# Layer 2's LayerNorm computed by token rows, and most of it placed beside the first image's attention

## The chip, the cores and the metric

The kernel runs on one core of a Trainium2 chip. The metric is the time of one execution on the device in microseconds (us). Five engines of the core have queues of their own: TensorE (PE; its weight loads are shown as PEld), VectorE (DVE), ScalarE (ACT), GpSimd (POOL) and SyncE (SP, which only issues transfers). On each engine instructions run in the order of its queue, and semaphores make them wait for other engines.

## The reference, cut to what matters

A batch of 4 images with 256 channels and 32 x 32 positions passes four layers. Layer 0 is a state-space block, layer 1 an attention-like convolution, layer 2 attention and a mixture of experts, layer 3 linear attention and an LSTM-like recurrence over 1,024 steps. The change lies between the end of layer 0 and the end of layer 2's attention:

```python
def _ln_t(v, eps=1e-5):
    m = jnp.mean(v, axis=-1, keepdims=True)
    s = jnp.var(v, axis=-1, keepdims=True)
    return (v - m) / jnp.sqrt(s + eps)

# layer 1: f = theta phi / N ; y = f g ; w_y = conv1x1(y), normalised over the batch
    return w_y + x
# layer 2
t = _to_tokens(x)                     # (4, 1024, 256): a token is a position
t = t + _L2_attn_ref(_ln_t(t), ...)   # one head of width 256, softmax over 1024 tokens
t = t + _L2_ffn_ref(_ln_t(t), ...)    # the experts
```

Because theta, phi and g of layer 1 have one output channel, its output w_y is, for each channel, a scale and an offset applied to one row theta of the image. The scale and offset need statistics over all four images; with them, the residual of one image does not depend on the others. Layer 2's LayerNorm and attention are independent for each image.

## The kernel before, in words

The activations x stay in SBUF with channels on the partitions: two chunks of 128 channels, 4 images, 1,024 positions each (`s.x`). All arithmetic is in fp32. T is 4,096 tokens; `NBLK` = 8 blocks of W = 512 tokens; `TPI` = 8 tiles of 128 tokens in an image; `BPI` = 2 blocks of 512 in an image.

*Order of the work.* The kernel is written on a framework that inserts the semaphores and lists each engine's instructions in an order of its own, within the dependencies. `_in_order` adds ordering without a semaphore between the instructions of one engine. Tiles come from pools with a number of buffers (`bufs`); a new tile in a used buffer waits for the readers of the old one, and so does a tile of a new pool in memory that a closed pool had. [...]one tile `[P, W]` is a bank. Two engines that read the same PSUM tile do so one after the other, in the order of the source.

*Layer 1* (`_layer1`, L546 to L659). TensorE forms theta, phi and g rows (L582), ScalarE and VectorE take statistics (L586 to L594), a product with ones sums them over the partitions (L605), and some thirty small VectorE instructions give the offset `off` and the coefficient `coef` (L610 to L644), among them `_rsqrt`, a reciprocal root in 13 steps. Then, image by image, the theta row is spread over the partitions by a product (L649), scaled by ScalarE into `wy` (L654), and added to x by VectorE (L659).

*Layer 2's LayerNorm* (`_layernorm`, L190 to L222) works with channels on the partitions. For each of the eight blocks a product with 1/256 gives the mean on all partitions (L202), VectorE subtracts it (L203), ScalarE squares (L205), and a second product collects the variance of the block in one of eight rows (L207). After the last block, ScalarE takes the root (L215), VectorE the reciprocal (L217), and for each block a product spreads the row over the partitions (L221) and VectorE multiplies (L222). The result is `u`, for all images.

*Layer 2's weights* (`_layer2_weights`, L678) are combined by small products (L703 to L709) and copied by VectorE (L710 to L717) while layer 1 ends.

*Layer 2's attention* (`_layer2_attention`, L759 to L860). For each image: four blocks of queries (L789, copied by ScalarE at L794), eight tiles of values (L801, L805), then eight tiles of 128 queries. A tile has four score products (L814), a row maximum on VectorE (L822 to L824), the exponential on ScalarE (L828), the division on VectorE (L832, L833), and eight transposes in two groups of four (L838), one copied by ScalarE (L845) and one by VectorE (L843). After four tiles, two times eight products with the values (L850) and an addition to x (L855). Score tiles `p_s`, transposed tiles `p_t` and the other products `p_mm` have two PSUM tiles each, eight banks together.

Beside the attention of images 1 to 3 goes the routing head of the image before (`_head`), a generator: after each step it yields, and `beside(n)` in the attention loop takes n steps, 11 for each tile of 128 queries and so 88 in an image. What is left is taken at the image's end (L856). Image 0 has no such parts: L778 gives it an empty iterator. The head begins with transposes of x into token rows (L874), statistics (L877, L880) and a copy into `rows` (L878).

*The experts* (`_layer2_experts`) follow, with transfers issued by POOL; small tables for them are computed by VectorE (`_table`, `_pick`, `_count`, `_part_tiles`), in tiles of the pool `m.one`. Layer 3 comes last and is the longest part.

Of the kernel before, what the change touches and what calls it, by code (L numbers as in the profile page):

```python
# [11 lines left out]
F32 = mybir.dt.float32  # L12
# [7 lines left out]
P = 128  # L20
B = 4
# [62 lines left out]
def _setup(s):  # L84
# [30 lines left out]
    s.avg_row = s.const.tile([P, 2 * NBLK - 1], F32, name="avg_row")  # L115
    nc.vector.memset(s.avg_row, 0.0)
    nc.vector.memset(s.avg_row[:, NBLK - 1 : NBLK], 1.0 / D)

    s.spread = s.const.tile([NBLK, NBLK, P], F32, name="spread")
    nc.vector.tensor_copy(s.spread, _bc(s.ident[:NBLK, :NBLK], 2, P))  # L120

# [68 lines left out]
def _layernorm(s, u):  # L190

    nc = s.nc
    with ExitStack() as ctx:
        pool = ctx.enter_context(s.tc.tile_pool(name="ln", bufs=2))
        ps = ctx.enter_context(s.tc.tile_pool(name="ln_ps", bufs=2, space=PSUM))
        ps1 = ctx.enter_context(s.tc.tile_pool(name="ln_ps1", bufs=1, space=PSUM))
        var = ps1.tile([NBLK, W], F32, name="var")
        for i in range(NBLK):
            t = bass.ts(i, W)
            mean = ps.tile([P, W], F32, name="mean")  # L200
            for k in range(C):
                nc.tensor.matmul(mean, s.avg, s.xt[:, k, t], start=k == 0, stop=k == C - 1)  # L202
            nc.vector.tensor_sub(u[:, :, t], s.xt[:, :, t], _bc(mean, 1, C))  # L203
            sq = pool.tile([P, C, W], F32, name="sq")
            nc.scalar.activation(sq, u[:, :, t], AF.Square)  # L205
            for k in range(C):
                nc.tensor.matmul(  # L207
                    var,
                    s.avg_row[:, NBLK - 1 - i : 2 * NBLK - 1 - i],
                    sq[:, k, :],  # L210
                    start=i == 0 and k == 0,
                    stop=i == NBLK - 1 and k == C - 1,
                )
        std = pool.tile([NBLK, W], F32, name="std", bufs=1)
        nc.scalar.activation(std, var, AF.Sqrt, bias=s.eps[:NBLK])  # L215
        rstd = pool.tile([NBLK, W], F32, name="rstd", bufs=1)
        nc.vector.reciprocal(rstd, std)  # L217
        for i in range(NBLK):
            t = bass.ts(i, W)
            wide = ps.tile([P, W], F32, name="wide")  # L220
            nc.tensor.matmul(wide, s.spread[:, i, :], rstd, start=True, stop=True)  # L221
            nc.vector.tensor_mul(u[:, :, t], u[:, :, t], _bc(wide, 1, C))  # L222
# [323 lines left out]
def _layer1(s):  # L546
# [4 lines left out]
    with ExitStack() as ctx:  # L551
        keep = ctx.enter_context(tc.tile_pool(name="l1_keep", bufs=1))
        pool = ctx.enter_context(tc.tile_pool(name="l1", bufs=2))
        ps = ctx.enter_context(tc.tile_pool(name="l1_ps", bufs=1, space=PSUM))
        wide = ctx.enter_context(tc.tile_pool(name="l1_wide", bufs=2, space=PSUM))
# [13 lines left out]
        spread = keep.tile([P, B, P], F32, name="spread")  # L569
# [4 lines left out]
        rows = keep.tile([P, BPI, W], F32, name="rows")  # L574
        stats = keep.tile([P, BPI, nc.vector.BN_STATS_DIM], F32, name="stats")
        dot = keep.tile([P, BPI], F32, name="dot")
        for i in range(BPI):
            p = [ps.tile([P, W], F32, name=f"p_{j}") for j in range(2)]
            for j in range(2):
                for k in range(C):  # L580
                    for b in range(B):
                        nc.tensor.matmul(  # L582
                            p[j][bass.ts(b, R), :], w[:, j, k, :], s.x[:, k, b, bass.ts(i, W)],
                            start=k == 0, stop=k == C - 1, tile_position=(0, R * b),
                        )
            nc.scalar.activation(rows[:, i, :], p[0], AF.Identity, bias=bias)  # L586
            nc.vector.bn_stats(stats[:, i, :], rows[:, i, :])
            prod = pool.tile([P, W], F32, name="prod")
            nc.vector.scalar_tensor_tensor(
                prod, p[1], s.row["g_b"], rows[:, i, :], ALU.add, ALU.mult,  # L590
                accum_out=dot[:, i : i + 1],
            )
# [11 lines left out]
        p = ps.tile([P, 3, B], F32, name="p_own")  # L604
# [30 lines left out]
        coef = keep.tile([P, B, C], F32, name="coef")  # L635
        nc.vector.tensor_mul(coef, _bc(d, 2, C), _bc(scale, 1, B))

        off = keep.tile([P, C], F32, name="off")
# [7 lines left out]
        for b in range(B):  # L646
            theta = wide.tile([P, BPI, W], F32, name="theta")
            for i in range(BPI):
                nc.tensor.matmul(  # L649
                    theta[:, i, :], spread[:, b, :], rows[:, i, :], start=True, stop=True  # L650
                )
            for c in range(C):
                wy = pool.tile([P, L], F32, name="wy")
                nc.scalar.activation(  # L654
                    wy, theta.rearrange("p i w -> p (i w)"), AF.Identity,
                    bias=off[:, c : c + 1], scale=coef[:, b, c : c + 1],
                )
                xs = s.x[:, c, b, :]
                nc.vector.tensor_add(xs, xs, wy)  # L659
# [60 lines left out]
def _layer2(s):  # L720
# [4 lines left out]
    with ExitStack() as ctx:  # L725
# [28 lines left out]
        m.counts = None  # L754
        _layer2_attention(s, m)
# [3 lines left out]
def _layer2_attention(s, m):  # L759
    nc, tc = s.nc, s.tc  # L760
    scale = D**-0.5
    with ExitStack() as ctx:
        keep = ctx.enter_context(tc.tile_pool(name="l2_keep", bufs=1))
        u = keep.tile([P, C, T], F32, name="u")
        with tc.tile_pool(name="l2_w", bufs=1) as w_pool:
            with tc.tile_pool(name="l2_w_ps", bufs=1, space=PSUM) as w_ps:
                w = _weights(s, w_pool, "w_l2")
                _layernorm(s, u)
# [8 lines left out]
        for b in range(B):  # L777
            parts = _head(s, m, b - 1, psum) if b > 0 else iter(())  # L778
# [264 lines left out]
def _table(s, m, name, n, tiles):  # L1043
# [5 lines left out]
    t = lambda shape, x: m.one.tile(shape, F32, name=f"{name}_{x}")  # L1049
# [15 lines left out]
def _pick(s, m, name, mine, values):  # L1065
# [3 lines left out]
    w = m.one.tile([P, n, K], F32, name=f"{name}_w")  # L1069
    nc.vector.tensor_mul(w, mine, _bc(values, 1, n))  # L1070
    of = m.one.tile([P, n], F32, name=f"{name}_of")
# [4 lines left out]
def _weight_rows(s, m, name, expert):  # L1076
# [3 lines left out]
    row = m.one.tile([P, n], F32, name=f"{name}_row")  # L1080
# [6 lines left out]
def _count(s, m, name, values, n, size, least):  # L1087

    nc = s.nc
    edges = m.one.tile([P, n], F32, name=f"{name}_edges")  # L1090
    nc.vector.tensor_scalar(edges, m.marks[:, :n], float(size), float(least), ALU.mult, ALU.add)
    over = m.one.tile([P, E, n], F32, name=f"{name}_over")
    nc.vector.tensor_tensor(over, _bc(values, 2, n), _bc(edges, 1, E), ALU.is_ge)
    held = m.one.tile([P, E], F32, name=f"{name}_count")
# [4 lines left out]
def _taken(s, m, name, n, first, tiles):  # L1099

    nc = s.nc
    taken = m.one.tile(list(tiles.shape), F32, name=f"{name}_taken")
# [5 lines left out]
def _first_tiles(s, m):  # L1108
# [7 lines left out]
    base = m.one.tile([P, E], F32, name="f_base")  # L1116
# [11 lines left out]
def _part_tiles(s, m, name, n, A, tiles, start, ahead):  # L1128
# [9 lines left out]
    if K > E:  # L1138
        over = m.one.tile([P, n], F32, name=f"{name}_over")
# [5 lines left out]
    base = m.one.tile([P, K], F32, name=f"{name}_base")  # L1145
# [4 lines left out]
    at = m.one.tile([P, n, A], F32, name=f"{name}_at")  # L1150
    nc.vector.tensor_tensor(at, _bc(own, 2, A), _bc(s.token[:, :A], 1, n), ALU.add)
    counts = m.one.tile([P, K], F32, name=f"{name}_counts")
# [4 lines left out]
    valid = m.one.tile([P, n, A], F32, name=f"{name}_valid")  # L1157
# [15 lines left out]
    places = m.one.tile([P, n * A], F32, name=f"{name}_ahead")  # L1173
# [8 lines left out]
def _other_tiles(s, m):  # L1182
# [5 lines left out]
    tiles = m.one.tile([P, 2 * E], F32, name="m_tiles")  # L1188
    start = m.one.tile([P, 2 * E], F32, name="m_start")
# [8 lines left out]
    begin = m.one.tile([P, E], F32, name="h_start")  # L1198
# [4 lines left out]
    left = m.one.tile([P, E], F32, name="h_left")  # L1203
# [3 lines left out]
    total = m.one.tile([P, 1], F32, name="h_total")  # L1207
# [7 lines left out]
def _layer2_experts(s, m):  # L1215
# [9 lines left out]
    with ExitStack() as body:  # L1225
        wp = body.enter_context(tc.tile_pool(name="moe_w", bufs=2))
        hp = body.enter_context(tc.tile_pool(name="moe_h", bufs=2))
        rp = body.enter_context(tc.tile_pool(name="moe_r", bufs=3))
# [367 lines left out]
def _layer3_lstm(s, x, u_l3, lam, q, wq, constants):  # L1596
# [295 lines left out]
    _setup, _layer0, _layer1, _layer2, _layer3,  # L1892
# [92 lines left out]
```

## Time and profile before

| what | us |
|---|---|
| median of 3 runs (3392.86 to 3399.31) | 3398.27 |
| the profiled execution, its own time | 3408.06 |
| its span, first to last instruction | 3406.3 |
| layer 1's first product to its offset | 343.06 to 359.10 |
| layer 1's residual, all images | 359.1 to 370.2 |
| layer 2's LayerNorm, all images | 370.2 to 422.2 |
| attention of image 0 | 422.2 to 508.2 |
| attention of image 1, with image 0's head | 508.2 to 596.4 |
| attention of image 2, with image 1's head | 596.4 to 685.2 |

Over the whole span TensorE is busy 93%, VectorE 59%, ScalarE 36%, POOL 11%. The mean granted TensorE clock is 0.973 of full speed. All durations below come from one profiled execution. In the tables of stages, a number in brackets after x is a count of records; an fp32 matmul is recorded twice and a transpose once. The chain of waits follows the work that ended last from instruction to instruction back through what released each. A line in a group table ends with the idle time of the engine just before such instructions and what ended it.

### The profile page before, as it was taken

Reading aid. Unit: us, or ns where it says so; the run is one execution under the profiler, and the core shown is the slowest. Engines: PE = TensorE matmul, PEld = TensorE weight load, DVE = VectorE, ACT = ScalarE, POOL = GpSimd, SP = SyncE. Lnnn points to the kernel's source line nnn. Section 1 sums busy time; section 2 is a strip of 40 time slices with the busy share of each in tenths; the row PEclk is TensorE's granted clock in tenths of the full one; section 3 lists DMA queues with packets and bytes.
Section 4 is the critical chain, followed back from the end, with each engine's and each line's share of the span. In section 5 each row is a group of like instructions: output and inputs, shape, how many; then the busy total and the mean of one; then the engine's idle time right before and its main releaser. Section 6 shows DMA issues by size and latency. Waiting matters only on the chain.

```text
span 3406.3 us, 146430 instructions
## 1 busy us (share of the span) xinstructions
PE 3177.1 (93%) x65186; PEld 2489.1 (73%) x65186; DVE 1997.0 (59%) x8389; ACT 1233.9 (36%) x5057; POOL 378.8 (11%) x468
## 2 busy tenths in 40 slices
PE   7788899998899996999999999999999999999888
PEld 4465344446788884688888888888888888888776
DVE  5696534452211115557777777776777767776666
ACT  4633222223222222433434334343343343443333
POOL 0083002223433330000000000000000000000000
PEclk9899899999999997999999999999999999999999
DMA  1291001115555654000000000000000000000000
GB/s 69 67 298 34 10 0 38 38 36 203 187 195 206 230 212 148 0 3 5 4 11 4 5 11 4 11 4 4 11 4 5 10 4 5 10 5 4 10 4 10
DMA packets 78058, 180.50 MB, mean 53 GB/s; under 512 B 6256, under 2 KB 63920, under 8 KB 72816
## 3 DMA queue, kind: packets, MB, share of 16 engines
q0 software_dynamic: 14880, 106.99, 8.5%
q1 hardware_dynamic: 60624, 59.12, 5.9%
q8 instruction: 511, 8.37, 1.0%
q10 hardware_dynamic: 1920, 5.00, 0.4%
q14 instruction: 123, 1.01, 0.1%
HBM read 111.26 MB, written 59.84 MB: 50 GB/s over the span
## 4 chain that ended last, share of the span: by engine, by line
PE 72%; DVE 14%; ACT 5%; issue 3%; DMA 2%; POOL 1%; ACTq 0%; DVEq 0%; POOLq 0%
PE p_c L1826 11%; PE p_c L1817 8%; PE ph L1300 6%; PE po L1334 6%; DVE turned L1867 6%; PE p_i L1817 5%; PE p_o L1826 5%; PE p_i L1826 5%; PE p_o L1817 5%; PE beside L1767 4%; PE p_mm L850 3%; PE p_s L814 2%; ACT a_o L1868 2%; DVE x L1880 2%; ACT th L1878 1%
## 5 line engine op out<-in xcount | busy, mean ns | idle before, releaser
L1868 ACT ACTIVATE add<-turned 128x8 f32<-128x8 f32 x1024 | 214.3, 209 | 1011.4 <-DVE turned L1867 1011.4
L1826 PE MATMUL p_c<-w_v,x 128*4 128x64 f32 x16368 | 416.7, 219 | 60.6 <-DVE x L1880 57.9
L1817 PE MATMUL p_c<-xg,shift 128*128 128x64 f32 x2048 | 446.0, 299 | 0.0
L1826 PE MATMUL p_o<-w_v,x 128*4 128x64 f32 x16368 | 417.8, 219 | 0.0
L1826 PE MATMUL p_i<-w_v,x 128*4 128x64 f32 x16368 | 417.4, 219 | 0.0
L1817 PE MATMUL p_i<-xg,shift 128*128 128x64 f32 x2048 | 407.7, 281 | 0.0
L1867 DVE STREAM_TRANSPOSE turned<-p_c 128x64 f32<-128x64 f32 x1024 | 255.7, 250 | 253.9 <-PE p_c L1826 220.0
L1817 PE MATMUL p_o<-xg,shift 128*128 128x64 f32 x2048 | 396.4, 275 | 0.0
L1817 PEld LDWEIGHTS p_c<-xg,shift 128*128 128x128 f32 x2048 | 304.9, 188 | 117.6 <-DVE turned L1867 0.4
L1826 PEld LDWEIGHTS p_c<-w_v,x 128*4 128x4 f32 x16368 | 227.9, 85 | 180.8 <-DVE x L1880 102.0
L1880 DVE TENSOR_TENSOR x<-a_o,th 128x8 f32<-128x8 f32 x1024 | 171.2, 167 | 246.0 <-ACT th L1878 246.0
L1817 PEld LDWEIGHTS p_o<-xg,shift 128*128 128x128 f32 x2048 | 311.4, 192 | 0.0
L1817 PEld LDWEIGHTS p_i<-xg,shift 128*128 128x128 f32 x2048 | 305.1, 188 | 0.0
L1826 PEld LDWEIGHTS p_o<-w_v,x 128*4 128x4 f32 x16368 | 281.9, 87 | 0.8 <-issue 0.5
L1826 PEld LDWEIGHTS p_i<-w_v,x 128*4 128x4 f32 x16368 | 281.6, 87 | 0.3
L1867 DVE STREAM_TRANSPOSE turned<-p_i 128x64 f32<-128x64 f32 x1024 | 271.9, 266 | 0.9 <-PE p_i L1826 0.7
L1292 ACT ACTIVATE hT<-ph,w 128x256 f32<-128x256 f32 (+1 forms) x288 | 131.3, 465 | 355.8 <-PE ph L1300 267.3
L1300 PE MATMUL ph<-uT,w 128*128 128x256 f32 x1056 | 241.6, 386 | 19.6 <-DVE uT L1279 11.3
L1867 DVE STREAM_TRANSPOSE turned<-p_o 128x64 f32<-128x64 f32 x1024 | 255.6, 250 | 0.9 <-PE p_o L1826 0.3
L1334 PE MATMUL po<-w,hT 128*128 128x256 f32 x1104 | 251.1, 380 | 2.7 <-ACT hT L1292 1.5
L1868 ACT ACTIVATE a_o<-turned 128x8 f32<-128x8 f32 x1024 | 213.3, 208 | 95.4 <-DVE cell L1871 4.5
L1300 PEld LDWEIGHTS ph<-uT,w 128*128 128x128 f32 x1056 | 203.2, 194 | 50.2 <-DVE uT L1279 12.1
(499 smaller groups left out, 4395.0 us busy)
## 6 DMA issues: line engine op xcount, KB each, us to landing
sorted<-zeros SPq DMA_DIRECT2D x32, 1032.0 KB
y_in<-results SPq DMA_DIRECT2D x16, 512.0 KB
x<-in_x_dram SPq DMA_DIRECT2D x8, 512.0 KB
tokens<-rows SPq DMA_DIRECT2D x4, 1024.0 KB
x<-tokens SPq DMA_DIRECT2D x8, 512.0 KB
out_dram<-x_l SPq DMA_DIRECT2D x64, 64.0 KB
results<-y,place POOLq DMA_INDIRECT x69
w_l<-in_w_l_dram ACTq DMA_DIRECT2D x1, 1092.0 KB
```

The costliest lines, as they stand in the source:

```text
L814: nc.tensor.matmul(p_s[:, h, :], q[:, k, q0 : q0 + P], u[:, k, b * L + h * W : b * L + (h + 1) * W], start=k == 0, stop=k == C - 1,)
L850: nc.tensor.matmul(p, v[:, n, bass.ts(c, P)], prT[:, n, :], start=n == 0, stop=n == TPI - 1,)
L1292: nc.scalar.activation(hT[:, n, : A * P], ph, AF.Gelu, bias=b1[:, n : n + 1])
L1300: nc.tensor.matmul(ph, w1[:, k, bass.ts(n, P)], uT[:, k, :], start=k == 0, stop=k == C - 1,)
L1334: nc.tensor.matmul(po, hT[:, n, bass.ts(a, P)], w2[:, n, :], start=n == 0, stop=n == NHC - 1,)
L1767: nc.tensor.matmul(p[bass.ts(i, R), :], rows[:, k, bass.ts(g, R)], w_u[:, k, at : at + GQ // GC], start=k == 0, stop=k == C - 1, tile_posi ...
L1817: nc.tensor.matmul(p[:, :H], shift[:, row * B : row * B + P], xg[n][:, g, bass.ts(i, H)], start=True, stop=t == 0,)
L1826: nc.tensor.matmul(p[R * i : R * i + B, :H], hs[:, t - 1, bass.ts(k, B)], w_v[:, k, i * GQ + g * H : i * GQ + (g + 1) * H], start=False, s ...
L1867: nc.vector.transpose(zt.rearrange("p c w -> p (c w)"), pz[g][:, :H])
L1868: nc.scalar.activation(dst.rearrange("p (c b) -> p c b", c=C), zt[:, :, :B], f)
L1878: nc.scalar.activation(th, cell[:, :, 1], AF.Tanh)
L1880: nc.vector.tensor_mul(h, a_o, th)
```

## The change

*Layer 2's LayerNorm* becomes `_norm_parts`, a generator for one image. It transposes two tiles of 128 tokens at a time into one PSUM tile, so that tokens are on the partitions; ScalarE copies the rows to SBUF, VectorE takes mean and variance of each row (`bn_stats`, `bn_aggr`). After four such groups come `_rsqrt` on all eight tiles at once and the negative product of mean and root (`shift`); ScalarE scales the eight tiles of rows in place; they are transposed back in four groups of four, and VectorE copies each to `u`. `rows` is the tile that the heads use too, from `m.one`, with one buffer.

*Layer 1* no longer adds its residual. It returns a generator `parts(b, psum)` that does so for one image in two halves of 512 positions. What this needs later (`l1_spread`, `l1_rows`, `l1_coef`, `l1_off`) lies in a pool `norm` that lives through the attention. `_layer1` is now called from `_layer2_attention`, after the load of layer 2's weights is issued; it is no longer a phase of its own.

*Placement.* Image 0's residual and norm run ahead of the attention, in four PSUM tiles of their own, with VectorE's instructions held in the order of the source. Those of images 1 to 3 become the parts beside image 0's attention, where there were none: 28 steps an image, 84 in all, in the banks of `p_mm`.

*Tables.* The small tables of the experts go to a pool `m.tables`, which is `m.one` for the first tiles and a pool of the experts' stage afterwards. The constants `avg_row` and `spread` of the old norm go.

```diff
-    s.avg_row = s.const.tile([P, 2 * NBLK - 1], F32, name="avg_row")
-    nc.vector.memset(s.avg_row, 0.0)
-    nc.vector.memset(s.avg_row[:, NBLK - 1 : NBLK], 1.0 / D)
-
-    s.spread = s.const.tile([NBLK, NBLK, P], F32, name="spread")
-    nc.vector.tensor_copy(s.spread, _bc(s.ident[:NBLK, :NBLK], 2, P))
...
-def _layernorm(s, u):
...
+def _norm_parts(s, pool, one, u, b, psum):
+    nc = s.nc
+    mv = pool.tile([P, TPI, 2], F32, name="mv")
+    rows = one.tile([P, TPI, 2, ROW], F32, name="rows")[:, :, 0, :D]
+    for n in range(0, TPI, 2):
+        p = psum()
+        for i in range(2):
+            for k in range(C):
+                at = i * D + k * P
+                nc.tensor.transpose(
+                    p[:, at : at + P], s.x[:, k, b, bass.ts(n + i, P)], s.ident
+                )
+        yield
+        nc.scalar.copy(rows[:, n : n + 2, :], p.rearrange("p (n d) -> p n d", n=2))
+        stats = pool.tile([P, 2, nc.vector.BN_STATS_DIM], F32, name="stats")
+        for i in range(2):
+            nc.vector.bn_stats(stats[:, i, :], p[:, bass.ts(i, D)])
+        for i in range(2):
+            nc.vector.bn_aggr(mv[:, n + i, :], stats[:, i, :])
+        yield
+    rstd = pool.tile([P, TPI], F32, name="rstd")
+    for i, _ in enumerate(_rsqrt(s, pool, rstd, mv[:, :, 1])):
+        if i % 4 == 3:
+            yield
+    shift = pool.tile([P, TPI], F32, name="shift")
+    nc.vector.scalar_tensor_tensor(shift, mv[:, :, 0], -1.0, rstd, ALU.mult, ALU.mult)
+    yield
+    for n in range(TPI):
+        nc.scalar.activation(
+            rows[:, n, :], rows[:, n, :], AF.Identity,
+            bias=shift[:, n : n + 1], scale=rstd[:, n : n + 1],
+        )
+        if n % 4 == 3:
+            yield
+    for i in range(BPI):
+        for c in range(C):
+            p = psum()
+            for j in range(TPB):
+                nc.tensor.transpose(
+                    p[:, bass.ts(j, P)], rows[:, i * TPB + j, bass.ts(c, P)], s.ident
+                )
+            yield
+            nc.vector.tensor_copy(u[:, c, b * L + i * W : b * L + (i + 1) * W], p)
+            yield
...
-def _layer1(s):
+def _layer1(s, after):
...
-        for b in range(B):
-            theta = wide.tile([P, BPI, W], F32, name="theta")
-            for i in range(BPI):
-                nc.tensor.matmul(
-                    theta[:, i, :], spread[:, b, :], rows[:, i, :], start=True, stop=True
-                )
+    def parts(b, psum):
+        for i in range(BPI):
+            p = psum()
+            nc.tensor.matmul(p, spread[:, b, :], rows[:, i, :], start=True, stop=True)
+            yield
+            wy = after.tile([P, C, W], F32, name="wy", bufs=2)
             for c in range(C):
-                wy = pool.tile([P, L], F32, name="wy")
                 nc.scalar.activation(
-                    wy, theta.rearrange("p i w -> p (i w)"), AF.Identity,
+                    wy[:, c, :], p, AF.Identity,
                     bias=off[:, c : c + 1], scale=coef[:, b, c : c + 1],
                 )
-                xs = s.x[:, c, b, :]
-                nc.vector.tensor_add(xs, xs, wy)
+            yield
+            xs = s.x[:, :, b, bass.ts(i, W)]
+            nc.vector.tensor_add(xs, xs, wy)
+            yield
...
-            with tc.tile_pool(name="l2_w_ps", bufs=1, space=PSUM) as w_ps:
+            with ExitStack() as early:
+                w_ps = early.enter_context(tc.tile_pool(name="l2_w_ps", bufs=1, space=PSUM))
                 w = _weights(s, w_pool, "w_l2")
-                _layernorm(s, u)
+
+                residual = _layer1(s, norm)
+                first_ps = early.enter_context(tc.tile_pool(name="l2_first", bufs=4, space=PSUM))
+                start = len(nc.cur_bb.bb.instructions)
+                for part in (residual, lambda b, p: _norm_parts(s, norm, m.one, u, b, p)):
+                    for _ in part(0, lambda: first_ps.tile([P, W], F32, name="p")):
+                        pass
+                _in_order(s, start, (mybir.EngineType.DVE,))
                 _layer2_weights(s, w, keep, w_ps)
...
-            parts = _head(s, m, b - 1, psum) if b > 0 else iter(())
+            if b > 0:
+                parts = _head(s, m, b - 1, psum)
+            else:
+                parts = chain(*(
+                    part for i in range(1, B)
+                    for part in (residual(i, psum), _norm_parts(s, norm, m.one, u, i, psum))
+                ))
...
-    t = lambda shape, x: m.one.tile(shape, F32, name=f"{name}_{x}")
+    t = lambda shape, x: m.tables.tile(shape, F32, name=f"{name}_{x}")
...
+        m.tables = body.enter_context(tc.tile_pool(name="moe_tables", bufs=1))
...
-    _setup, _layer0, _layer1, _layer2, _layer3,
+    _setup, _layer0, _layer2, _layer3,
```

## The prediction

> **What bounds the kernel now.** I read the busy time of the engines by stage first, because the page's averages mix a recurrence of 2,000 us with the short stages that the change touches. The columns are each engine's busy microseconds and, at the end, the granted TensorE clock, DMA share and GB/s.
>
> ```profile
> 343.06:359.10 16.04, 15.23 (x107) 8.09 (x106) 10.55 (x50) 1.37 (x2) 0.00 (x0) 1.00 0.12 47
> 359.10:370.20 11.10, 5.95 (x8) 2.28 (x8) 8.19 (x7) 9.20 (x8) 0.00 (x0) 0.66 0.00 0
> 370.20:403.50 33.30, 31.79 (x64) 9.19 (x64) 12.02 (x31) 10.41 (x10) 0.24 (x1) 0.91 0.00 1
> 403.50:422.20 18.70, 13.93 (x16) 4.23 (x17) 13.11 (x9) 0.00 (x0) 0.00 (x0) 0.59 0.00 0
> 422.20:508.20 86.00, 81.23 (x241) 41.47 (x242) 30.02 (x59) 18.14 (x29) 0.00 (x0) 0.95 0.00 0
> 508.20:596.40 88.20, 84.11 (x280) 43.59 (x279) 41.91 (x129) 23.67 (x46) 17.65 (x24) 0.96 0.10 36
> ```
>
> The rows are layer 1's statistics, its residual, the norm's first pass (mean, centring, squares, variance), its second pass (reciprocal, spread, product), the attention of image 0, and that of image 1 with a routing head beside it. 343.06 to 422.2 is 79 us in which almost nothing else runs. In image 0's attention TensorE is busy for 81.2 of 86.0 us, while VectorE (30.0) and ScalarE (18.1) have room. So TensorE's own work, and waits in it, set the price of what is put beside it.
>
> The chain of waits gives the limits inside the stages (start, length, what):
>
> ```profile
> 350.13 1.91 PE theta L649 x4
> ...
> 399.14 3.62 PE var L207 x8
> ...
> 403.50 3.35 DVE rstd L217
> ...
> 406.89 13.94 PE wide L221 x16
> ...
> 422.23 9.72 PE p_mm L789 x16
> 431.95 7.12 PE p_mm L801 x32
> ...
> 461.82 13.73 PE p_mm L850 x32
> ...
> 492.72 15.49 PE p_mm L850 x32
> 508.21 6.87 PE p_mm L789 x16
> ```
>
> L789 costs 9.72 us in image 0 and 6.87 in image 1: TensorE arrives cold, at the half clock of the row before (0.59). L850 costs 13.73 and then 15.49 us; what lies before the slow one is in the waits of that stage (total, times, longest):
>
> ```profile
> PE p_t L838 <- DVE pr L833: 3.6, 2, 3.4
> ```
>
> One wait of 3.4 us cost 15.49 - 13.73 = 1.8 us more in the matmuls behind it.
>
> Durations, from the groups of 420 to 700 us:
>
> ```profile
> L838 PE MATMUL p_t<-ident,pr 128*128 128x128 f32 x192 | 27.2, 288 | 11.8 <-DVE pr L833 11.8
> L843 DVE COPY prT<-p_t 128x512 f32<-128x512 f32 x24 | 16.5, 686 | 6.5 <-PE p_t L838 6.1
> L845 ACT COPY prT<-p_t 128x512 f32<-128x512 f32 x24 | 14.0, 583 | 70.6 <-PE p_t L838 65.3 <-issue 5.3
> L794 ACT ACTIVATE q<-p_mm,r 128x512 f32<-128x512 f32 x16 | 11.0, 687 | 88.7 <-PE p_mm L789 88.7
> L996 ACT ACTIVATE rows<-rows,shift,rstd 128x256 f32<-128x256 f32 x16 | 8.5, 592 | 2.3 <-DVE shift L908 2.3
> L877 DVE BATCH_NORM_STATS2 stats<-p_mm 128x6 f32<-128x256 f32 x16 | 6.5, 419 | 1.6 <-PE p_mm L874 1.4
> L880 DVE BATCH_NORM_AGGREGATE mv<-stats 128x2 f32<-128x6 f32 x16 | 2.8, 179 | 0.1
> ```
>
> A mean of 288 ns for a transpose includes its latency; eight take 0.87 us in the chain, so 0.109 us each at full clock. A matmul of 512 columns is two records, and the chain's 6.87 us for sixteen gives 0.86 us each. The residual's addition over 1,024 elements takes 1.22 us (L659), a step of the small reciprocal root 0.167 us, 0.2 with its gap (L1035 to L1039).
>
> **The change, part by part.** It removes the residual and norm of all images ahead of attention, adds image 0's alone there, and adds images 1 to 3 to image 0's attention.
>
> *Layer 1's statistics.* In the changed order the first of its products waits for the last of the four updates of x, which end at 341.60 + 2.73 = 344.33; before, it began at 343.06. That is 1.35 late; 7.07 us of products end at 351.45. Layer 2's small products now stand around the sum over partitions on TensorE's queue: 2.5 us before that sum, then 0.5, the two theta products of image 0 (1.9), and 0.95 + 0.45 + 0.5 to about 358.5. VectorE's copy of r waits for the last of these and now stands ahead of the root for the gain; behind it are 13 steps and some small copies, 3.5 us. The offset is ready at 362.05; before, at 359.1. Cost: 3 us.
>
> *Image 0's residual and norm.* ScalarE's two halves of 512 (0.69 each) and the addition: 362.05 + 1.4 + 1.25 = 364.7, the second addition 366.1. The norm has four groups of four transposes; each is copied by ScalarE (0.58) and then read by VectorE, two statistics (0.84) and two aggregates (0.36), 1.25 with gaps. The reads of one bank stand in order, so VectorE ends at 366.4 + 4 x 1.25 = 371.4. Root and shift, 14 x 0.2 = 2.8: 374.2. Eight scalings on ScalarE, 8 x 0.59 = 4.75: 379.0. The last transposes: 379.9. Attention began at 422.2, so 42.3 us are gained.
>
> Here a rule speaks against the change. The Trainium skill ("TensorE: Matmul & The Clock Gate", Part 1 and Part 4) says that an idle window of some 3.4 us halves the clock, and that transposes do not bring it back as matmuls do. The trace agrees with the first (0.66 and 0.59 in the sparse stages, and the 1.8 us above); no stage of it is transposes alone, so the second is open. By the rule the first attention product starts as cold as before (9.72 us); if transposes count, 2.85 us less. I take the rule: the new opening is sparse anyway.
>
> *Images 1 to 3 beside image 0.* Each adds to TensorE 2 theta products (1.72) and 32 transposes (3.5): 5.2, times three 15.6 us. To VectorE: two additions 2.44, statistics 4.8, root 2.8, four copies 2.75: 12.8, times three 38. To ScalarE: 2.8 + 2.3 + 4.75 = 9.8, times three 29.5. VectorE then has 68 us and ScalarE 48 us, neither the bound.
> The two ends: if all of it filled the waits, image 0 would take its warm TensorE work 76.0 + 15.6, the cold start 2.85 and the old waits 4.8, 99.3 us. If each image's chain (17.8 us by the steps above) stood exposed, 86.0 + 53.4 = 139.4.
> Between them I walked the three queues in the changed order with the durations above. Waits on TensorE up to the first half's value products: 7.7 us, mostly behind ScalarE's eight scalings of image 1, which stand ahead of copies of p_t, and behind a VectorE queue where the row maximum and the probabilities stand among the statistics. After these products, 5.3 us: statistics of image 3 hold back the last probabilities. The end is worst: image 3's sixteen final transposes stand directly ahead of the second half's value products. From its last statistics come root and shift (about 3.9 us with a copy between), eight scalings (4.75) and one copy, with nothing left for TensorE: 7.8 us, and 1.8 us of cold clock after it. Image 0 takes 76.0 + 15.6 + 2.85 + 7.7 + 5.3 + 7.8 + 1.8 = 117.0, which is 31.0 more.
>
> *Costed at nothing.* The constants that go from the set-up (0.8 us of VectorE) lie beside the load of x. SP's and POOL's queues keep their order, so no scatter, expert load or clearing of slots moves; the load of w_l2 stays behind the same ScalarE instruction and had landed by 346.5. Five table instructions on VectorE move from attention to the start of the experts, where the queue waits 9.1 us for rows; without that cover they cost 0.7. Images 1 to 3 keep their order and length.
>
> *Sum.* -42.3 + 31.0 = -11.3 us. The profiled execution took 3408.06 us for a span of 3406.3, 9.8 over the median; nothing in the part of the difference depends on that, so I take it from the median: 3398.27 - 11.3 = 3387.
>
> **The rivals.** *The parts fit better* (0.15). Image 3's norm ends earlier than walked, or transposes warm the clock. Image 0 takes about 105 us, gain 23: 3375. For it: heads beside images 1 to 3 cost only 2.2 us each. Against: those heads have no step that must end before the stage's last products.
> *The parts fit worse, no difference* (0.20). In VectorE's queue row maxima wait behind statistics that themselves wait for ScalarE's copies. At 121.5 to 135 us for image 0 the change is within 0.2% (6.8 us), about what a measurement of this kernel can tell from none; say 3396. The hops between engines of some 0.05 us, which I counted only along the longest path, lie in this direction.
> *The clock is lost, slower* (0.10). The place is image 0's attention: if waits of over 3.4 us recur there, its work runs at half clock and each warm microsecond costs another. Par is reached with 11.3 of its 91.6 us of work at half clock, a loss of 0.2% with 18; with 30 it is 3398 - 11 + 30 = 3417. Against: between the waits stand matmuls of over 0.8 us each, and before, only one wait of 3.4 us was seen there.
> That the parts are not beside attention is excluded by the order: they stand between the score products.
>
> **How the numbers follow.** The likeliest, 0.55, is 3387 with a range of its own of 3381 to 3391.5. With the better fit that is 0.70 faster; 0.20 the same, 0.10 slower. The range 3371 to 3400 leaves out most of the lost-clock case and the edge of the best.
>
> **What would show it.** The first attention product should begin about 36 us after layer 1's first one (before 79), its first sixteen records take about 9.7 us, and the attention of image 0 about 117 us; images 1 to 3 stay at 88 to 89. TensorE's longest wait should be on ScalarE's scaled rows of image 3, 5 us or more, and the value products behind it should take over 15 us. VectorE should show about 68 us of work in image 0. I am wrong if image 0 takes under 108 or over 125, if the opening takes over 45, or if the experts or the recurrence move.

## The result, and the profile after

The changed kernel takes 3377.11 us (median of 4 runs, 3376.62 to 3379.43) against 3397.45 for the kernel before beside it: a ratio of 0.9946, with a 95% interval of 0.9935 to 0.9958. That is 20.3 us less; the forecast was 11.3 us less, 3387, in a range of 3371 to 3400. In a second comparison, on a chip where every kernel was some 10 us slower, the ratio was 0.9950 (0.9937 to 0.9964). The direction and the range held; the size was too small by 9 us, and the experiments are about these 9.

The stages of the changed kernel, in the same columns as before: each engine's busy microseconds with its records, the granted TensorE clock, the DMA share and GB/s. The rows are layer 1's statistics up to the offset; image 0's residual and norm; the attention of image 0 with the parts of images 1 to 3; the attention of images 1 and 2 with heads.

```profile
345.31:362.18 16.87, 13.58 (x102) 7.15 (x102) 9.85 (x53) 1.38 (x3) 0.00 (x0) 0.97 0.05 18
362.18:379.68 17.50, 7.49 (x33) 5.53 (x33) 11.20 (x36) 9.17 (x16) 0.00 (x0) 0.64 0.00 0
379.68:488.77 109.09, 99.64 (x349) 54.90 (x350) 59.59 (x167) 44.60 (x77) 0.00 (x0) 0.92 0.00 1
488.77:575.74 86.97, 82.87 (x280) 43.17 (x279) 41.90 (x129) 23.69 (x46) 17.53 (x24) 0.98 0.11 37
575.74:663.40 87.66, 83.53 (x279) 43.30 (x278) 41.88 (x129) 23.76 (x46) 17.85 (x24) 0.96 0.11 37
```

From layer 1's first product to the first attention product it is 34.4 us where it was 79.2; image 0's attention takes 109.1 where it took 86.0. The second row also shows the 17.5 us that one image's residual and norm take when nothing lies beside them: TensorE is busy for 7.5 of these, VectorE for 11.2.

The chain of waits of the changed kernel (start, length, what), from image 0's opening to image 1:

```profile
364.94 1.13 PE p L194 x4
...
374.37 3.94 PE p L223 x15
378.33 1.30 DVE u L227 x2
379.68 7.13 PE p_mm L814 x16
...
433.48 13.97 PE p_mm L875 x32
...
466.41 0.61 ACT rows L213
467.06 1.97 PE p_mm L223 x7
...
472.40 16.37 PE p_mm L875 x32
488.77 6.87 PE p_mm L814 x16
```

L814, L875 and L223 are the attention's first products, the value products and the transposes of the scaled rows. Three things stand here. The first attention products take 7.13 us, not the 9.72 of before. The first half's value products begin 53.8 us after the attention's first product; the forecast had 7.7 us of waits in that half. And the second half's value products stand behind ScalarE's scaling (L213) of image 3's rows and take 16.37 us instead of 13.97.

The waits of TensorE in image 0's attention (total, times, longest):

```profile
PE p_mm L223 <- ACT rows L213: 3.8, 1, 3.8
PE p_t L863 <- DVE pr L858: 1.6, 1, 1.6
PE p_mm L194 <- DVE top L849: 1.5, 1, 1.5
...
PE p_mm L223 <- DVE u L227: 0.7, 1, 0.7
PE p_s L839 <- ACT pr L853: 0.6, 1, 0.6
```

Of the lines shown, only the last lies ahead of the first half's value products. TensorE idles 109.09 - 99.64 = 9.45 us in the stage, not 20.8.

### The profile page after: what moved, and what is told of

It is laid out like the page before. It is cut to its first block, busy times and chain, and to the rows that moved or that the text cites. A ratio compares the mean times of both kernels' runs of the same rounds, so it can differ in the third digit from the quotient of the medians.

```text
span 3375.1 us, 146707 instructions
## 1 busy us (share of the span) xinstructions
PE 3143.6 (93%) x65234; PEld 2485.6 (74%) x65234; DVE 2007.4 (59%) x8505; ACT 1253.3 (37%) x5103; POOL 378.3 (11%) x468
## 4 chain that ended last, share of the span: by engine, by line
PE 71%; DVE 14%; ACT 5%; issue 3%; DMA 2%; POOL 1%; ACTq 0%; DVEq 0%; POOLq 0%
PE p_c L1852 11%; PE p_c L1843 8%; PE ph L1326 6%; DVE turned L1893 6%; PE po L1360 6%; PE p_i L1843 5%; PE p_i L1852 5%; PE p_o L1852 5%; PE p_o L1843 5%; PE beside L1793 4%; PE p_mm L875 3%; PE p_s L839 2%; ACT a_o L1894 2%; DVE x L1906 2%; ACT th L1904 1%
## 6 DMA issues: line engine op xcount, KB each, us to landing
w_l<-in_w_l_dram ACTq DMA_DIRECT2D x1, 1092.0 KB, 11.3
```

## The experiments

### The kernel before, once more

The first two profiled executions differ by 31.2 us in their spans, of which only 19.4 are there at the start of image 1's attention; 7 more appear in the experts' stage. This run asks whether the change did that.

> The kernel before once more, for a second profiled execution of it. In the first pair of profiles the changed kernel gained 19.4 us up to the start of image 1's attention, 7 us more in the stage of the experts (first expert product to layer 3's first product: 542.5 us before, 535.3 after) and 3 us behind that. Theory 1, the change moves only the stages around the norm, and the rest is the difference between two executions: this execution shows about 535 us in the experts' stage, a span near 3396, and 422.2 us (within 2) for the start of the first attention product. Theory 2, the change of pools for the tables or the earlier start speeds up the experts: this execution shows 542 again.

The chain of waits of this execution, the first attention products of images 0 and 1:

```profile
419.74 9.32 PE p_mm L789 x16
...
505.12 6.87 PE p_mm L789 x16
```

The experts' products, by their tile (least, median and largest duration in ns, first and last start, form):

```profile
L1300 PE MATMUL ph<-uT,w x1056: 378/379/797, 780.0 to 1279.2; 128*128 128x256 f32 x176
...
L1322 PE MATMUL ph<-ident,raw x24: 272/273/329, 1131.3 to 1291.3; 128*128 128x128 f32 x24
```

From the first to the last of these it is 1291.3 - 780.0 = 511.3 us. In the first execution of before it was 519.2, in that of the changed kernel 512.1. Later, on the other chip, the changed kernel took 520.6 there and a version of it 519.3. So these 7 us go with the execution or the chip, not with the kernel: theory 1. The stage of the norm varies too. From layer 1's first product to the first attention product it took 76.2 us here and 79.2 in the first profile, so that this product came at 419.74, 2.5 us ahead of the expected 422.2. Over the two executions of each kernel, the time from layer 1's first product to image 1's first attention product was 165.15 and 161.55 us before, and 143.46 and 145.44 after. The difference of the means is 18.9 us, near the 20.3 of the medians.

### All images ahead of the attention

```diff
-                for part in (residual, lambda b, p: _norm_parts(s, norm, m.one, u, b, p)):
-                    for _ in part(0, lambda: first_ps.tile([P, W], F32, name="p")):
-                        pass
+                for b in range(B):
+                    for part in (residual, lambda b, p: _norm_parts(s, norm, m.one, u, b, p)):
+                        for _ in part(b, lambda: first_ps.tile([P, W], F32, name="p")):
+                            pass
...
-                parts = chain(*(
-                    part for i in range(1, B)
-                    for part in (residual(i, psum), _norm_parts(s, norm, m.one, u, i, psum))
-                ))
+                parts = iter(())
```

> Residual and norm by token rows of all four images stand ahead of the attention, none beside it; nothing is left out. Theory 1, the gain comes from the place beside the attention and not from working by token rows: image 0's opening took 17.5 us as one chain with one buffer of rows, so each further image takes 14 to 17.5 us in the open, 42 to 52 in all; image 0's attention falls from 109 to about 84. Sum +17 to +27, so 3394 to 3404, about the kernel before. Theory 2, the row form is the gain in itself: images follow each other at the rate of VectorE's work, some 11 us, so 33 us more, less 25, and the time is about 3385 or under, half of the gain or more kept.

It takes 3409.09 us (5 runs), a ratio of 1.0037 (1.0023 to 1.0052) to the kernel before: slower than it, and above the 3394 to 3404 of theory 1. The stages of this kernel, image 0's own opening, images 1 to 3's, and the attention of image 0 without parts:

```profile
360.90:379.60 18.70, 10.20 (x36) 6.92 (x36) 11.10 (x36) 10.61 (x18) 0.00 (x0) 0.52 0.00 0
379.60:429.37 49.77, 24.04 (x106) 14.84 (x105) 33.10 (x109) 25.81 (x46) 0.00 (x0) 0.70 0.00 0
429.37:514.53 85.16, 80.65 (x241) 41.61 (x242) 30.01 (x59) 18.16 (x29) 0.00 (x0) 0.96 0.00 0
```

Each further image costs 49.77 / 3 = 16.6 us in the open, as theory 1 had it, and image 0's attention falls from 109.1 to 85.2. The sum is 49.8 - 23.9 = 25.9 us over the changed kernel, as forecast for the stages; the medians of the two comparisons are 32 apart, and these 6 us more stay open. The profiled execution (span 3415.9) has 14 us more behind the experts' stage, 2114 us for 2100, with a granted clock of 0.968 for 0.976 over the span. The run of the earlier tail below shows 2114 there too, and both profiled executions were 9 us over the median of their kernel, so this is not taken for an effect of the order. The chain of waits between two images:

```profile
389.37 0.61 ACT rows L213
...
390.02 3.14 PE p L223 x12
...
395.73 1.00 PE p L655 x2
396.75 1.46 ACT wy L659 x2
```

The next image's theta products (L655) stand in TensorE's queue behind the last transposes of the image before (L223), which wait for its scaled rows (L213). So the row form alone gains nothing in this arrangement. Another order, or a second buffer of rows, was not tried. The gain of the change is the place: three images cost 23 us beside the attention and 50 ahead of it.

### The tail, later

```diff
-                    beside(4)
+                    beside(3 if b == 0 else 4)
...
-                    beside(3)
+                    beside(2 if b == 0 else 3)
```

> Beside image 0's attention 9 steps for each tile of 128 queries instead of 11, so that the last 12 steps, with image 3's scalings and its sixteen last transposes, come behind the second half's value products in the source; nothing is left out. Theory 1, the 3.8 us wait on image 3's scaled rows and the 2.6 us of cold clock in the value products behind it are the price of the tail: both go, image 0 takes 102.5 to 104, the second value products about 13.8 us, and the time is 3371. Theory 2, the chain of image 3's norm has its length wherever it ends: TensorE then waits for it behind the value products or in image 1, and the time stays within 2 us of 3377.

3374.48 us (4 runs), a ratio to before of 0.9940 (0.9923 to 0.9956). The chain of waits of this version in image 0:

```profile
379.65 7.13 PE p_mm L814 x16
...
427.60 13.75 PE p_mm L875 x32
...
464.10 15.41 PE p_mm L875 x32
...
480.27 0.67 PE p_mm L223 x4
481.71 0.66 PE p_mm L223 x4
482.37 7.13 PE p_mm L814 x16
```

Image 3's last transposes now stand behind the second value products, and the wait on its scaled rows falls from 3.8 to 0.2 us. Image 0 takes 102.7 us, 6.4 less, as theory 1 said; the time is 3.5 us over its 3371. The value products take 15.4 and not 13.8: ahead of them stand only shorter waits (1.4 us the longest), and still the granted clock is 0.50 from 463.6 to 467.0 us.

> The changed kernel once more, beside the version with the later tail on one chip and for a second profile. Both theories: image 0's attention 109 us (within 2; the first product 7.1 or 9.1 us), the time 3377 (within 3). In the first comparison the later tail was measured apart from it, 3374.48 against 3377.11.

> The version with 9 steps for each tile, measured beside the changed kernel. Theory 1, the 6.4 us that image 0 lost there less the 1.6 that image 1 gained are kept: 4 to 6 us under the changed kernel. Theory 2, the gain is given back behind the attention: within 2 us of it.

Side by side, with five runs each, the changed kernel takes 3389.80 us and this version 3386.72, on the slower chip, so that the expected 3377 could not be met; the ratios to before are 0.9950 (0.9937 to 0.9964) and 0.9939 (0.9925 to 0.9952). The sign is the same in both comparisons, but the intervals overlap: 3 us are at the edge of what can be measured, under the 4 to 6 expected. Part of image 0's 6.4 us is given back in image 1, as the expectation had already counted; what else is missing stays open. Image 1 takes 88.58 us in this version and 86.99 in the changed kernel, 1.6 more in both pairs of profiles; 1.3 of it are value products of image 1, here in the changed kernel (first line) and in this version (second line):

```profile
561.17 14.57 PE p_mm L875 x32
555.02 15.93 PE p_mm L875 x32
```

The same wait of 3.41 us on the probabilities stands ahead of both. But the granted clock behind it is 0.50 from 559.1 to 562.5 us in the changed kernel and from 552.3 to 559.1 in the later tail, 3.4 us or 6.8. The kernel before has 6.8 us there too (577.7 to 584.5) and 15.86 us of value products. So this difference is how long the clock stayed down after the same wait; why it stayed longer was not tested.

The second profile of the changed kernel missed the first by 2: image 0 took 111.08 us. Its first attention products took 9.10 us where the first execution has 7.13, after the same sixteen transposes. What brings the clock back is the matter of two runs below.

### The tail, earlier in the source

```diff
-                    beside(4)
+                    beside(5 if b == 0 else 4)
...
-                    beside(3)
+                    beside(4 if b == 0 else 3)
```

> Beside image 0's attention 13 steps for each tile instead of 11, so that all 84 steps are named in the source before the last tile; nothing is left out. In the resulting order of TensorE's queue the score products run ahead, and all of image 3's steps (its two theta products, sixteen transposes to rows and sixteen back) stand between the last score products and the second half's value products. Theory 1, what counts is how much of image 3's chain TensorE meets with no other work: the opening's 17.5 us chain less its own TensorE work of 5.2, so about 12 us of waits instead of 6, with a cold clock behind it: image 0 takes 115 to 120 and the time is 3383 to 3388. Theory 2, steps named earlier end earlier: the tail wait goes, 3371.

3386.43 us (6 runs), a ratio to before of 0.9970 (0.9957 to 0.9982). The stage of image 0's attention, and in it the stretch from the first to the second half's value products:

```profile
376.39:492.73 116.34, 102.66 (x349) 55.59 (x350) 59.52 (x167) 44.19 (x77) 0.00 (x0) 0.91 0.00 1
444.09:478.03 33.94, 24.88 (x80) 12.81 (x81) 14.36 (x42) 9.84 (x18) 0.00 (x0) 0.82 0.00 0
```

Image 0 takes 116.3 us, as theory 1 had it, with a longest wait of 5.1 us on image 3's scaled rows; 2.0 of the 116.3 are a cold first product. The same work, named earlier in the source, ended later: the score products ran ahead, and between 457.9 and 478.0 us TensorE has none left to lie between the steps of image 3's chain.

### What brings the clock back

Two runs fill the 3.8 us in which TensorE waits for image 3's scaled rows. The first uses transposes of the identity, the second uses two products, both held behind the last transposes of probabilities. Each was executed once.

```diff
+                    if b == 0 and i == BPI - 1 and j == TPB - 1:
+                        fill = ps.tile([P, BPI, W], F32, name="p_s")
+                        for n in range(16):
+                            d = nc.tensor.transpose(fill[:, n // 8, bass.ts(n % 4, P)], s.ident, s.ident)
...
                     beside(3)
```

> The changed kernel with 16 transposes of the identity in TensorE's queue between the last transposes of probabilities of image 0 and the transposes of image 3's scaled rows, in the 3.8 us in which TensorE waits; their output is not used, nothing is left out. At half clock they take 16 x 0.21 = 3.4 us. Theory A, transposes don't count as work for the clock: the value products behind still take 16 us or more, image 0 stays at 109. Theory B, transposes count (in the changed kernel the clock came back during the sixteen transposes ahead of the attention): the value products take 13.8 to 14.6 us, image 0 106 to 107.5.

> The same gap filled by two products of 128x128 with 512 columns (1.7 us each at half clock) in place of the transposes; their output is not used, nothing is left out. Theories A and B both: TensorE's work is then without a gap from 461 us on, the clock is back before the value products, which take 13.8 to 14.6 us; image 0 takes 106 to 107.5. If they still take 16, it is not the gap that costs the clock.

TensorE's instructions in time with the transposes (start, length, line, in brackets the idle time before it; L874 is the filling, L886 the value products):

```profile
462.59 1.97 PE L863 MATMUL p_t<-ident,pr 128*128 128x128 f32 x8 [1.63 <-DVE pr L858]
464.36 3.62 PE L874 MATMUL p_s<-ident 128*128 128x128 f32 x16
468.39 1.91 PE L223 MATMUL p_mm<-ident,rows 128*128 128x128 f32 x8 [0.42 <-ACT rows L213]
471.07 1.27 PE L223 MATMUL p_mm<-ident,rows 128*128 128x128 f32 x8 [0.77 <-DVE u L227]
473.02 14.00 PE L886 MATMUL p_mm<-prT,v 128*128 128x512 f32 x32 [0.67 <-DVE u L227]
```

The stretches of that kernel; the granted clock is the third number from the end:

```profile
465.00:467.00 2.00, 2.00 (x11) 2.00 (x11) 1.73 (x11) 0.00 (x0) 0.00 (x0) 0.50 0.00 0
467.00:469.00 2.00, 1.58 (x8) 0.95 (x7) 0.54 (x4) 1.26 (x3) 0.00 (x0) 0.60 0.00 0
469.00:473.02 4.02, 2.48 (x14) 1.36 (x15) 2.03 (x4) 2.79 (x6) 0.00 (x0) 1.00 0.00 0
```

With the products in their place:

```profile
463.31 3.62 PE L874 MATMUL p_s<-u,ident 128*128 128x512 f32 x4
...
471.97 14.00 PE L886 MATMUL p_mm<-prT,v 128*128 128x512 f32 x32 [0.67 <-DVE u L227]
```

Theory B. The clock went from 0.50 to 1.00 between 467 and 469 us, while TensorE had done nothing but transposes since 462.6, and the value products took 14.0 us in both kernels instead of 16.4. Transposes and products did the same for the clock. Image 0 took 105.84 us with the products, just under the expected 106. With the transposes it took 107.99, of which 2.2 are a cold first product.

The opening shows the same without any filling. These are stretches of the changed kernel with the sixteen transposes ahead of the attention (374.37 to 378.33) and behind them, and the whole opening of its second execution:

```profile
374.30:377.00 2.70, 2.63 (x11) 1.62 (x12) 0.64 (x2) 2.70 (x7) 0.00 (x0) 0.50 0.00 0
378.40:379.68 1.28, 0.03 (x2) 0.00 (x1) 1.22 (x2) 0.00 (x0) 0.00 (x0) 1.00 0.00 0
...
362.00:379.57 17.57, 7.80 (x33) 5.60 (x33) 11.19 (x36) 9.16 (x16) 0.00 (x0) 0.50 0.00 0
```

In the first execution the clock came back under these transposes, at 378.2 us, and the first attention products took 7.13 us. In the second it came back only at 383.6 us, within these products, and they took 9.10.

### VectorE's and ScalarE's room

The last two runs add work that nobody uses to the parts of images 1 to 3: statistics on VectorE, or scalings on ScalarE. Each was executed once.

```diff
+        if b > 0:
+            again = pool.tile([P, 2, nc.vector.BN_STATS_DIM], F32, name="again")
+            for i in range(2):
+                nc.vector.bn_stats(again[:, i, :], p[:, bass.ts(i, D)])
```

> For images 1 to 3 each group of rows has its two statistics taken twice on VectorE, the second result unused: 24 more of them, 9 us more of VectorE's work beside image 0 (0.38 us each, as they overlap in pairs), which brings VectorE from 59.6 to about the 68 us of the forecast. Nothing is left out. Theory 1, TensorE's own work sets the price and VectorE has room: up to the first half's value products (53.8 us in the changed kernel, of which TensorE waits 0.6) at most 1.5 us more, in the tail 1 to 2.5 us more for image 3's chain. Theory 2, the forecast's 7.7 us of waits in that half were missing only because VectorE's work was overestimated by 8 us: the half takes 59 or more, image 0 117 or more.

The stages of that kernel up to the first half's value products, and the whole of image 0:

```profile
376.68:436.34 59.66, 54.93 (x201) 30.65 (x201) 38.10 (x104) 26.51 (x44) 0.00 (x0) 0.96 0.00 1
...
376.68:488.60 111.92, 99.35 (x349) 54.17 (x350) 65.61 (x191) 44.78 (x77) 0.00 (x0) 0.95 0.00 1
```

Neither theory holds whole. The first half takes 59.66 us, of which 2.1 are the cold first product; TensorE idles 59.66 - 54.93 = 4.7 us in it, against 0.8 in the changed kernel. The cold start is not the reason: the second execution of the changed kernel has it too and idles 0.8 us in that half. So 6 us more on VectorE (59.6 to 65.6; the forecast's 68 was not reached) do reach TensorE there, against theory 1. But image 0 as a whole takes 111.9 us, or 109.8 without the cold start, and not 117. The second value products came back to 13.97 us: TensorE's longest wait, 6.3 us for probabilities, now fell earlier, and the clock was back at 473.1 us, before these products began. What was lost early was gained late.

```diff
+    rows, again = both[:, :, 0, :D], both[:, :, 1, :D]
...
+        if b > 0:
+            nc.scalar.activation(
+                again[:, n, :], rows[:, n, :], AF.Identity,
+                bias=shift[:, n : n + 1], scale=rstd[:, n : n + 1],
+            )
```

> For images 1 to 3 each of the eight scalings is done twice on ScalarE, the first time into an unused half of the tile: 24 x 0.505 = 12 us more of ScalarE's work beside image 0. Nothing is left out. Theory 1, ScalarE has room as well, and only the tail is a chain: up to the first half's value products at most 1.5 us more, the tail's wait on image 3's scaled rows 4 us longer, image 0 about 113 to 115 (with the first product at 7.1 us). Theory 2, the forecast's waits behind the eight scalings of image 1 were real and only shortened, as a scaling takes 0.505 us and not 0.59: with twice the scalings the first half takes 58 us or more.

The same stages of this kernel, and TensorE's waits (total, times, longest) between the two halves' value products:

```profile
378.55:436.90 58.35, 56.85 (x215) 32.14 (x216) 37.74 (x99) 32.65 (x56) 0.00 (x0) 1.00 0.00 1
...
378.55:494.46 115.91, 102.00 (x349) 55.37 (x350) 60.23 (x167) 56.19 (x101) 0.00 (x0) 0.90 0.00 1
```

```profile
PE p_mm L229 <- ACT rows L219: 8.8, 4, 6.5
```

The first half's 58.35 us would speak for theory 2, were it not for the records: twelve more of TensorE's (215 for 203) were placed ahead of the value products, 3.9 us of busy time, and its idle time is 1.5 us, only 0.7 more. The added work changed the order of TensorE's queue, so the halves can be compared by their idle time only. The tail is where the 12 us of ScalarE tell: 8.8 us of waits on the scaled rows instead of 3.8, and 115.9 us for image 0, a little over the 113 to 115 of theory 1. So the waits "behind ScalarE's eight scalings of image 1" of the forecast were not there, and doubling the scalings did not make them.

The move of the tables was not tried alone.

## Why the prediction was right, and where it was wrong

*The opening.* Right. The attention began 42.5 us earlier (379.68 for 422.23); the forecast had 42.3. The offset came at 362.18 for 362.05, and the chain behind it at its pace.

*The first attention products.* The step took the rule of the Trainium skill ("TensorE: Matmul & The Clock Gate", Part 4) that transposes don't bring the clock back: 9.72 us. For the fp32 transposes of this kernel the runs contradict it. In the changed kernel the products took 7.13 us with only sixteen transposes directly ahead of them, and the filled gap shows the clock coming back under transposes alone. But the 2.85 us that the forecast named as the alternative are not sure either: of ten profiled executions with the same sixteen transposes directly ahead, in the changed kernel and its versions, five have 7.13 us and five 9.10 to 9.30. The same page, Part 1, says that the clock is decided by an activity window that runs freely; two outcomes for one sequence agree with that, though no run here sets the window's phase.

*The parts beside image 0.* The mechanism was right, the sum of waits wrong. This is the step that failed: "Waits on TensorE up to the first half's value products: 7.7 us". There were 0.6. With "after these products, 5.3 us", which were about 3.5, and the end's 7.8, which were 5.1, the forecast's 20.8 us of waits became 9.45 of idle time. TensorE was busy for 52.99 of the 53.80 us of that half. Part of it is that VectorE was busy for less: 59.6 us and not 68. The forecast added the lengths of records, and in the changed kernel these do add up to 67.3 us; but they overlap (24 statistics took 9.1 us, 0.38 each, where 0.42 was counted). The run with twice the statistics shows that such work does bring back about 4 us of waits in this half. The eight scalings had no such effect, so that reason was wrong. Which work hid the rest of the walk's waits was not taken apart further.

*TensorE's own work.* It was undercounted. Busy time was foreseen as 76.0 + 15.6 + 2.85 + 1.8 = 96.25 us and was 99.64, although the cold start was all but absent. A first 0.6 is in the sum itself: the 81.2 us of before less 2.85 and 1.8 are 76.6, not 76.0. In the changed kernel the clock was 0.50 from 460.1 to 477.2 us. That cost some 2.6 us in the value products (16.37 for 13.75) and some 3 in the three groups of eight transposes ahead of them, which took 1.97, 2.17 and 1.94 us where eight take 0.87 to 1.1 at full clock. So the same work at full clock is estimated at 94 us. The later tail, with 1.7 us of cold value products in 97.14, gives 95.5. Either is over the 91.6 of the forecast, by 2.4 to 3.9 us. Groups of four transposes stand at 0.44 to 0.67 us in the chains, where 0.44 was counted; that this is the whole difference was not shown.

*The tail.* Right in kind, and shown by the moves in both directions: longer than 15 us of value products (16.4), behind a wait on image 3's scaled rows that is the longest of the stage. It was 3.8 us and not 5 to 8, as a scaling follows the other after 0.505 us (eight in 4.04), not 0.59.

*The sum.* 23.1 us for image 0 where 31.0 stood, 7.9 of the 9 by which the time was missed. Two errors stood against each other here: 11.35 us of waits too many and 3.4 us of TensorE's busy time too few. That image 0 stayed above the 108 us under which the forecast called itself wrong, by 1.1 us in the first execution, is partly luck. The rest of the 9 is within what two executions of one kernel differ by. Of the rivals, the better fit was the nearest in time (105 us and 3375). Both of its reasons came, a warm clock at the start and an earlier end of image 3's norm, but the first half's missing 7.1 us of waits were more than these two. Behind image 0 little moved: image 1 took 87.0 us in both executions of the changed kernel and 88.2 and 88.1 in those of before, which goes with the clock behind its wait on the probabilities as told under the later tail.

## What to carry to other kernels

Work that is moved beside a stage bound by TensorE costs TensorE's own busy time and whatever chain ends last in that stage; the waits that I counted by walking the queues hop by hop were twice those that came. Part of that was adding up the lengths of records that overlap. Put the end of a moved chain where its consumer is far: three counts of steps per tile, for the same work, gave 102.7, 109.1 and 116.3 us for this stage, and the one with the steps earliest in the source was the worst. Compare stages over at least two executions before a difference outside the change is explained.

## What the hardware showed

Transposes in fp32 brought TensorE's clock back as products did: 3.62 us of either in the same gap brought the value products behind from 16.4 to 14.0 us. The same transposes ahead of image 0's attention gave 7.13 or 9.1 to 9.3 us for the same sixteen records, five times each, so that about 2 us of a stage's time can be chance. After the same wait of 3.41 us in image 1 the clock stayed at half for 3.4 us in one kernel and for 6.8 in another, 1.3 us of value products apart. And the experts' stage of one kernel took 511 or 519 us in different executions, which is more than a third of what this change moved.
